# Graph attention on one core: the last batch's output summed on TensorE, and the last tile's masks placed in PSUM first

## The chip, the core and the metric

The kernel runs on one core of a Trainium2 chip. The metric is the device time of one execution in microseconds (us). Beside it stands a profile of one execution: the span from its first to its last instruction, and what each engine did in it. The engines are TensorE (PE; PEld is its weight load), VectorE (DVE), ScalarE (ACT), GpSimd (POOL) and SyncE (SP), which here only issues transfers. Each works through its own instructions in order and waits on semaphores for the others.

## The reference, cut to what matters

Sixteen batches (B), each with N = 512 nodes of F = 512 features, attend to their first 20 nodes, in two directions d, with 16 heads of 32 features. All inputs are float32.

```python
q_exp = jnp.where(row_zero[..., None], 0.0, q[:, None, :])
self_feat = jnp.concatenate([v, q_exp], -1) @ W_self.T + b_self
output = self_feat
for d in range(2):
    A = (adj_f if d == 0 else jnp.swapaxes(adj_f, 1, 2))[:, :, :20, :]
    cond = A.sum(-1)
    vb = A @ w_bias + b_bias
    kv = self_feat[:, :20]
    qh = (self_feat @ Wq[d].T + bq[d]).reshape(B, N, 16, 32)
    kh = (kv @ Wk[d].T + bk[d]).reshape(B, 20, 16, 32)
    aff = jnp.einsum('bnhd,bmhd->bnhm', qh, kh) / np.sqrt(32)
    aff = jnp.where(cond[:, :, None, :] > 0, aff, -9e15) + vb[:, :, None, :]
    w = softmax(aff, -1)
    out_t = jnp.einsum('bnhm,bmf->bnhf', w, kv)
    output += einsum('bnhf,hgf->bnhg', out_t, Wout[d]).reshape(B, N, 512) + bout[d]
return v + relu(output)
```

## The kernel before

**Setup.** Weights are folded: keys are brought into feature space (`g`), so that a score is one product of the self features with `g`; values (`vd`) already contain `Wout`. The biases `b_self` and `bout` are summed into `bo`, one number per output feature.

**Batches and tiles.** The main loop runs over batches `b` and over four tiles `nt` of 128 nodes. Everything is held with features on partitions: `xs[b]` and `sfs[b]` (self features without bias) are 128 partitions x 4 chunks x 512 nodes. A pass of the loop issues the products of the self features for later tiles (`self_feat`, L189), in pass 2 the attention of the batch before (`attend`, L314) and its output (`finish`, L327 and L333; `residual`, L336; `store`, L341), and then `scores` (L249) for this tile. There is no scheduler: the order in the source is the order on each engine, and the pools of tiles add waits.

**Scores and softmax.** A tile's scores fill two PSUM banks, one for each group `g` of 64 nodes; partitions are two halves of the heads times 64 nodes, and a bank's 320 columns are 8 heads x 40 neighbours (20 for each direction). One tile `ps_s` (pool `ps_s`, two buffers of two banks) holds both. `full` is the mask with the biases of that tile, made by POOL in `full_add` (L239) one pass ahead. `weigh` adds it to the scores in PSUM (L260), takes the maximum (L262) and subtracts it (L264); `expo` is the exponential on ScalarE (L269); in the next pass `normal` sums (L294), inverts (L295) and multiplies on POOL (L296), and `turn` (L303) transposes 32x32 blocks on VectorE into `wt`. For the last tile of the last batch, `weigh_half` and `turn_half` (L276 to L280, L285 to L288) do the same group by group and on VectorE.

**Attention.** `attend` multiplies `wt` with the values in 32x32 tiles of TensorE: 64 matmuls, which accumulate in pairs. Their results lie in four banks `q` (pool `ps_acc`, four buffers of one bank): `q // 2` gives the chunk pair, 0 and 1 or 2 and 3, and `q % 2` which 32 of every 64 nodes. Each bank is first written by a matmul with `start` set.

**The end.** The last batch has no successor, so its attention and output are written out after the loop, in two parts: tiles 0 to 2 (banks `most`), which wait for the transpose of tile 2, and tile 3 (banks `rest`), which waits for both halves of the last tile. VectorE adds the self features to the banks (L745), ScalarE adds `bo` and takes the ReLU (L749), POOL (L752) and VectorE (L755, L758) add `x`, and SP sends: three chunks of tiles 0 to 2 (L753), all chunks of tile 3 (L756), the fourth chunk (L759).

Of the kernel before, what the change touches and what calls it, by code (L numbers as in the profile page):

```python
# [13 lines left out]
P = 128  # L14
# [4 lines left out]
def gat_kernel(  # L19
# [224 lines left out]
    def scores(b, nt, g, ps):  # L244

        keys = gs[b].rearrange("p c (a w) -> p c a w", a=2)
        for k in range(C):
            for a in range(2):
                nc.tensor.matmul(  # L249
                    ps[bass.ts(a, R), g, : W // 2], sfs[b][:, k, bass.ds(nt * P + g * R, R)], keys[:, k, a],  # L250
                    start=(k == 0), stop=(k == C - 1),
                )
# [18 lines left out]
    def weigh_half(b, nt, ps, s, a):  # L271

        pw = ps[:, a, : W // 2]
        p3 = pw.rearrange("p (h m) -> p h m", m=NG)
        f = fulls[b, nt].rearrange("p g h m -> p g (h m)")[:, a]
        nc.vector.tensor_add(pw, pw, f)  # L276
# [28 lines left out]
    def attend(b, n, banks, tiles=slice(0, NT)):  # L305
# [3 lines left out]
        for i in range(2):  # L309
            for e in range(HL):  # L310
                j = n * HL * S // 32 + e * S // 32 + i
                for q in range(4):
# [4 lines left out]
                        start=(i == 0), stop=(i == 1),  # L317
# [314 lines left out]
    work = ctx.enter_context(tc.tile_pool(name="work", bufs=2))  # L632

    gs[0] = g0
    with tc.manual_schedule():
        load_keys(1)

# [3 lines left out]
        for b in range(B):  # L641
# [6 lines left out]

            for nt in range(NT):
# [21 lines left out]

                if prev is not None:
                    normal(*prev)
                ps = ps_s.tile([P, 2, 512], F32, tag="s", name=f"ps_s{b}_{nt}")
                for part in ahead(nt):
                    self_feat(*part)
                if nt == 2 and b > 0:
# [4 lines left out]
                    finish(b - 1, o, (0, 1), banks)  # L682
                for g in range(2):
                    scores(b, nt, g, ps)
# [11 lines left out]
                last = b == B - 1  # L696
                for part in ahead(nt):
                    self_copy(*part)
                if last and nt == NT - 1:
                    s = soft.tile(full, F32, tag="s", name=f"s{b}_{nt}", bufs=3)  # L700
                    weigh_half(b, nt, ps, s, 0)
                    turn(*prev)
                    weigh_half(b, nt, ps, s, 1)
                else:
                    s = weigh(b, nt, ps)
# [3 lines left out]
                if nt < NT - 1:  # L709
                    full_add(b, nt + 1)  # L710
# [16 lines left out]
        o = work.tile([P, C, N], F32, tag="o", name=f"o{b}")  # L727
        out_b = out[b].rearrange("(c p) n -> p c n", p=P)
        most = [ps_acc.tile([P, 512], F32, tag="acc", name=f"ps_o{b}_{q}") for q in range(4)]
        pairs = [ps_s.tile([P, 2, 512], F32, tag="s", name=f"ps_o{b}_{q}_2") for q in range(2)]  # L730
        rest = [pairs[q // 2][:, q % 2] for q in range(4)]
        parts = []
        for lo, hi, banks in ((0, NT - 1, most), (NT - 1, NT, rest)):
            width = (hi - lo) * R
            parts.append((slice(2 * lo, 2 * hi), slice(lo * P, hi * P), width, banks))
            for n in range(2):
                attend(b, n, [t[:, bass.ts(n, width)] for t in banks], slice(lo, hi))
        for ts, ns, width, banks in parts:
            for q in range(4):
                c = bass.ds(q // 2 * 2, 2)  # L740

                def of(t):
                    return t[:, c].rearrange("p c (t q n) -> p c t q n", q=2, n=32)[:, :, ts, q % 2]

                nc.vector.tensor_add(  # L745
                    of(o), banks[q][:, : 2 * width].rearrange("p (c t n) -> p c t n", c=2, n=32), of(sfs[b])
                )
            for c in range(C):
                nc.scalar.activation(o[:, c, ns], o[:, c, ns], AF.Relu, bias=bo[:, c : c + 1])  # L749
        ns = parts[0][1]  # L750
        for c in range(3):
            nc.gpsimd.tensor_add(o[:, c, ns], o[:, c, ns], xs[b][:, c, ns])  # L752
            nc.sync.dma_start(out_b[:, c, ns], o[:, c, ns])  # L753
        ns = parts[1][1]
        nc.vector.tensor_add(o[:, :, ns], o[:, :, ns], xs[b][:, :, ns])  # L755
# [50 lines left out]
```

## Time and profile before

| | |
|---|---|
| time, median of 3 runs (lowest to highest) | 634.22 us (633.94 to 636.79) |
| the profiled execution's own time | 634.41 us |
| its span | 632.6 us, mean granted TensorE clock 0.994 |
| busy, of the span | PE 98%, DVE 80%, POOL 53%, ACT 34% |
| chain that ended last | PE 85% (scores L249 43%, self features L189 33%, attention L314 6%) |
| the last batch's tile 2: scores on PE | start at 607.0 us |
| the last tile's second transpose on VectorE | 622.97 to 623.48 us |
| last send issued | 629.07 us |

"Busy" is the time in which an engine had an instruction of the program in work. The chain is followed back from the last instruction, at each step to what released it. A line of the timeline gives start, duration, engine, line of the kernel, operation, output and inputs, shape and count; in brackets how long the engine had idled and what ended that. The sum of an engine's durations can exceed its stretch a little, since instructions overlap at their ends. "Granted clock" is TensorE's clock as a share of full speed.

### The profile page before, as it was taken

How to read it: one execution, taken by the hardware profiler on the slowest of the kernel's cores; microseconds unless marked ns; L12 is line 12 of the kernel's file. 1: busy time of each engine (PE TensorE's matmuls, PEld its weight loads, DVE VectorE, ACT ScalarE, POOL GpSimd, SP SyncE). 2: the span in 40 equal slices, each digit the busy share in tenths (PEclk: the TensorE clock that was granted, in tenths of full speed). 3: DMA queues.
4: the chain of work that ended last, by engine and by line, in shares of the span. 5: the costliest groups of instructions: out<-in, count | busy, mean ns of one | idle time of the engine just before them, and what ended most of it. 6: DMA issues, size and time to landing. Idle time of an engine off the chain costs nothing.

```text
span 632.6 us, 16385 instructions
## 1 busy us (share of the span) xinstructions
PE 618.7 (98%) x6814; PEld 383.6 (61%) x6814; DVE 508.4 (80%) x815; ACT 218.1 (34%) x480; POOL 337.4 (53%) x258
## 2 busy tenths in 40 slices
PE   8999999999999999999999999999999999999993
PEld 6655459986565656565655656565656565656542
DVE  0566546879888888888888889797988888888886
ACT  1445321233342424242424233343334242424232
POOL 2405331446556464738392938474655646473853
PEclk9999999999999999999999999999999999999997
DMA  8999998628384565738392909292838465663322
GB/s 287 397 382 321 392 371 249 216 88 268 134 237 165 150 253 127 275 90 313 70 333 42 358 19 339 52 292 107 262 141 248 154 207 196 147 256 102 129 68 101
DMA packets 89569, 131.86 MB, mean 208 GB/s; under 512 B 8888, under 2 KB 59608, under 8 KB 87448
## 3 DMA queue, kind: packets, MB, share of 16 engines
q1 hardware_dynamic: 88824, 129.47, 61.7%
q0 software_dynamic: 672, 1.36, 0.8%
q8 instruction: 53, 0.87, 0.6%
q14 instruction: 20, 0.16, 0.1%
HBM read 90.89 MB, written 39.92 MB: 207 GB/s over the span
## 4 chain that ended last, share of the span: by engine, by line
PE 85%; DVE 2%; ACT 1%; issue 0%; DVEq 0%; ACTq 0%
PE ps_s L249 43%; PE ps_sf L189 33%; PE ps_o L314 6%; PE ps_v L523 1%; ACT o L749 0%; PE ps_nz L172 0%; DVE s L287 0%; DVE mx L278 0%; DVE o L745 0%; DVE s L279 0%; PE ps_g(3, 3, 0, 0, 2)0_778 L550 0%; PE ps_g(3, 2, 0, 1, 2)0_752 L550 0%; PE ps_g(3, 1, 1, 0, 2)0_724 L550 0%; PE ps_g(3, 0, 1, 1, 2)0_701 L550 0%; DVE ps_s L276 0%
## 5 line engine op out<-in xcount | busy, mean ns | idle before, releaser
L249 PE MATMUL ps_s<-g,sf 128*64 128x320 f32 x2048 | 287.6, 433 | 0.0
L249 PEld LDWEIGHTS ps_s<-g,sf 128*64 128x64 f32 x2048 | 155.4, 137 | 116.3 <-issue 6.2
L189 PE MATMUL ps_sf<-x,ws_v 128*64 128x256 f32 (+1 forms) x2048 | 222.0, 371 | 0.0
L189 PEld LDWEIGHTS ps_sf<-x,ws_v 128*64 128x64 f32 x2048 | 151.1, 137 | 67.5 <-issue 1.7
L296 POOL TENSOR_TENSOR s<-s,sm 128x640 f32<-128x640 f32 x63 | 80.1, 1271 | 145.5 <-DVE sm L295 134.8
L269 ACT ACTIVATE s<-s 128x640 f32<-128x640 f32 x63 | 46.5, 738 | 220.9 <-DVE s L264 220.9
L239 POOL TENSOR_TENSOR full<-cq,both 128x640 f32<-128x640 f32 x64 | 99.0, 1547 | 27.6 <-ACT both L230 23.5
L211 POOL TENSOR_TENSOR prod<-prod,wb_sb 128x880 f32<-128x880 f32 x32 | 61.3, 1915 | 56.5 <-ACT prod L210 56.5
L260 DVE TENSOR_TENSOR ps_s<-ps_s,full 128x640 f32<-128x640 f32 x63 | 52.3, 831 | 39.4 <-PE ps_s L249 39.4
L336 POOL TENSOR_TENSOR o<-o,x 128x512 f32<-128x512 f32 x60 | 75.5, 1281 | 0.0
L230 ACT COPY both<-add 64x80 f32<-64x80 f32 x128 | 32.8, 256 | 77.4 <-DVE add L225 76.3
L202 DVE SCALAR_TENSOR_TENSOR sf<-nz,qw,ps_sf 128x236 f32<-128x236 f32 (+1 forms) x128 | 52.6, 458 | 3.5 <-PE ps_sf L189 3.5
L333 ACT ACTIVATE o<-o,bo 128x512 f32<-128x512 f32 x60 | 40.0, 714 | 44.3 <-DVE o L327 44.3
L294 DVE TENSOR_REDUCE sm<-s 128x32 f32<-128x640 f32 x63 | 51.6, 818 | 4.4 <-ACT s L269 0.9
L262 DVE TENSOR_REDUCE mx<-ps_s 128x32 f32<-128x640 f32 x63 | 52.0, 825 | 2.2
L264 DVE TENSOR_TENSOR s<-ps_s,mx 128x640 f32<-128x640 f32 x63 | 51.9, 824 | 2.2
L303 DVE STREAM_TRANSPOSE wt<-s 128x640 f32<-128x640 f32 x63 | 52.5, 834 | 0.0
L314 PE MATMUL ps_o<-wt,vd 32*32 32x256 f32 (+2 forms) x2176 | 46.7, 381 | 4.2 <-issue 2.8
L314 PEld LDWEIGHTS ps_o<-wt,vd 32*32 32x32 f32 x2176 | 31.6, 104 | 19.8 <-issue 12.4
L327 DVE TENSOR_TENSOR o<-ps_o,sf 128x512 f32<-128x512 f32 x60 | 36.3, 668 | 0.0
L152 ACT ACTIVATE xn<-xn 128x512 f32<-128x512 f32 x56 | 34.3, 613 | 0.0
L216 DVE TENSOR_REDUCE cond<-adj 128x80 f32<-128x880 int32 x32 | 33.2, 1036 | 0.2 <-DMA adj<-in_adj 0.2
(205 smaller groups left out, 415.7 us busy)
## 6 DMA issues: line engine op xcount, KB each, us to landing
g<-g_d SPq DMA_DIRECT2D x15, 1280.0 KB, 9.0
g_d<-st SPq DMA_DIRECT2D x16, 1120.0 KB, 6.3
x<-in_xT SPq DMA_DIRECT2D x16, 1024.0 KB, 11.0
out_T<-o SPq DMA_DIRECT2D x61, 256.0 KB, 5.0
xn<-in_xn SPq DMA_DIRECT2D x28, 512.0 KB, 8.7
adj<-in_adj SPq DMA_DIRECT2D x32, 440.0 KB, 7.3
vd<-bd_d SPq DMA_DIRECT2D x64, 128.0 KB, 4.1
nz<-nz_d SPq DMA_DIRECT2D x14, 256.0 KB, 4.7
```

Of the source, the lines that this page charges most:

```text
L189: nc.tensor.matmul(held[0][bass.ts(a, R), i * N // 2 : i * N // 2 + hi - lo], ws_v[:, k, bass.ds((2 * f + i) * P + a * R, R)], xs[b][:, k, ...
L202: nc.vector.scalar_tensor_tensor(sfs[b][:, 2 * f + i, lo:hi], nzs[b][:, lo:hi], qw[:, 2 * f + i, b : b + 1], ps[:, i * N // 2 : i * N // 2 ...
L211: nc.gpsimd.tensor_mul(p, p, wb_sb.unsqueeze(1).to_broadcast([P, 2 * S, L]))
L239: nc.gpsimd.tensor_add(f, cqs[b].unsqueeze(1).to_broadcast(shape), adds[b, nt // 2][:, nt % 2].unsqueeze(2).to_broadcast(shape),)
L249: nc.tensor.matmul(ps[bass.ts(a, R), g, : W // 2], sfs[b][:, k, bass.ds(nt * P + g * R, R)], keys[:, k, a], start=(k == 0), stop=(k == C - 1),
L260: nc.vector.tensor_add(pw, pw, fulls.pop((b, nt)).rearrange("p g h m -> p g (h m)"))
L262: nc.vector.tensor_reduce(mx, p4, AX.X, ALU.max)
L264: nc.vector.tensor_sub(s, p4, mx.unsqueeze(3).to_broadcast(full))
L296: nc.gpsimd.tensor_mul(s, s, sm.unsqueeze(3).to_broadcast(full))
L303: nc.vector.transpose(wts[b][:, nt], s.rearrange("p a h m -> p (a h m)"))
L314: nc.tensor.matmul(banks[q][bass.ts(e, DH)].rearrange("p (t n) -> p t n", n=32), vds[b][r, e, i, q // 2 * 2 + n], wt[r, :, bass.ts(j, 32)] ...
L336: nc.gpsimd.tensor_add(o[:, c], o[:, c], xs[b][:, c])
```

## The change

- An identity matrix `ident` (128 x 128) is made on POOL in batch 1.
- In passes 0 and 1 of the last batch, ScalarE writes `biased` = self features + `bo`. POOL adds `x` to it: in chunks 0 and 1 for all nodes, in chunks 2 and 3 for the last tile's nodes only.
- For the last tile, each group of scores gets a bank of its own from `ps_acc`. `put_masks` writes the mask there by an identity matmul, and the scores accumulate on top; the mask add of `weigh_half` goes. The last mask sum is made on POOL one pass earlier, ahead of a `normal`.
- Each output bank of the last batch is started by `put_self`, an identity matmul of `biased`; `attend` accumulates on top (`start=False`). The one for bank 0 stands before the last tile's scores, the others behind them.
- Where the bank contains `x`, the output is the greater of bank and `x`, in one VectorE instruction: max(x + y, x) = x + relu(y). This holds for banks 0 and 1 of tiles 0 to 2 and all banks of tile 3. For banks 2 and 3 of tiles 0 to 2 ScalarE takes the ReLU from PSUM and POOL adds `x`.
- SP sends four pieces of two chunks each: tiles 0 to 2 (chunks 0 and 1, then 2 and 3), then tile 3 the same way. The output tile `o_last` takes a buffer of the keys, `biased` one of the outputs.

```diff
--- before.py
+++ after.py
@@ -241,14 +241,19 @@
             adds[b, nt // 2][:, nt % 2].unsqueeze(2).to_broadcast(shape),
         )
-    def scores(b, nt, g, ps):
+    def put_masks(b, nt, g, bank):
+        f = fulls[b, nt].rearrange("p g h m -> p g (h m)")
+        nc.tensor.matmul(bank[:, : W // 2], ident, f[:, g], start=True, stop=False)
+    def scores(b, nt, g, bank, start=True):
         keys = gs[b].rearrange("p c (a w) -> p c a w", a=2)
         for k in range(C):
             for a in range(2):
                 nc.tensor.matmul(
-                    ps[bass.ts(a, R), g, : W // 2], sfs[b][:, k, bass.ds(nt * P + g * R, R)], keys[:, k, a],
-                    start=(k == 0), stop=(k == C - 1),
+                    bank[bass.ts(a, R), : W // 2], sfs[b][:, k, bass.ds(nt * P + g * R, R)], keys[:, k, a],
+                    start=start and k == 0, stop=(k == C - 1),
                 )
     full = [P, 2, H, NG]
@@ -268,12 +273,9 @@
         sw = s.rearrange("p a h m -> p (a h m)")
         nc.scalar.activation(sw, sw, AF.Exp)
-    def weigh_half(b, nt, ps, s, a):
-        pw = ps[:, a, : W // 2]
-        p3 = pw.rearrange("p (h m) -> p h m", m=NG)
-        f = fulls[b, nt].rearrange("p g h m -> p g (h m)")[:, a]
-        nc.vector.tensor_add(pw, pw, f)
+    def weigh_half(b, nt, bank, s, a):
+        p3 = bank[:, : W // 2].rearrange("p (h m) -> p h m", m=NG)
         mx = soft.tile([P, H], F32, tag="mxh", name=f"mx{b}_{nt}{a}")
         nc.vector.tensor_reduce(mx, p3, AX.X, ALU.max)
         nc.vector.tensor_sub(s[:, a], p3, mx.unsqueeze(2).to_broadcast([P, H, NG]))
@@ -302,7 +304,7 @@
             wts[b] = work.tile([P, NT, W], F32, tag="wt", name=f"wt{b}")
         nc.vector.transpose(wts[b][:, nt], s.rearrange("p a h m -> p (a h m)"))
-    def attend(b, n, banks, tiles=slice(0, NT)):
+    def attend(b, n, banks, tiles=slice(0, NT), start=True, stop=True):
         wt = wts[b][:, tiles].rearrange("p t (g w) -> p (t g) w", g=2)
@@ -314,7 +316,7 @@
                     nc.tensor.matmul(
                         banks[q][bass.ts(e, DH)].rearrange("p (t n) -> p t n", n=32),
                         vds[b][r, e, i, q // 2 * 2 + n], wt[r, :, bass.ts(j, 32)],
-                        start=(i == 0), stop=(i == 1),
+                        start=start and i == 0, stop=stop and i == 1,
                     )
     def nodes(t, q):
@@ -630,10 +632,25 @@
     soft = ctx.enter_context(tc.tile_pool(name="soft", bufs=2))
     gp = ctx.enter_context(tc.tile_pool(name="gp", bufs=2))
     work = ctx.enter_context(tc.tile_pool(name="work", bufs=2))
+    ident = ctx.enter_context(tc.tile_pool(name="one", bufs=1)).tile([P, P], F32, name="ident")
     gs[0] = g0
     with tc.manual_schedule():
         load_keys(1)
+        def side(t, lo, hi, q):
+            v = t[:, bass.ds(q // 2 * 2, 2)].rearrange("p c (t q n) -> p c t q n", q=2, n=32)
+            return v[:, :, 2 * lo : 2 * hi, q % 2]
+        def of_bank(bank, lo, hi):
+            return bank[:, : 2 * (hi - lo) * R].rearrange("p (c t n) -> p c t n", c=2, n=32)
+        def put_self(banks, lo, hi, q):
+            nc.tensor.matmul(
+                of_bank(banks[q], lo, hi), ident, side(biased, lo, hi, q), start=True, stop=False
+            )
         prev = None
         o = None
@@ -646,6 +663,12 @@
                     return ((b, nt, 1),)
                 return ((b + 1, 0, 0), (b + 1, 1, 0)) if nt == 3 and b + 1 < B else ()
+            if b == 1:
+                nc.gpsimd.memset(ident, 0.0)
+                nc.gpsimd.affine_select(
+                    out=ident, in_=ident, pattern=[[-1, P]], compare_op=ALU.not_equal, fill=1.0,
+                    base=0, channel_multiplier=1,
+                )
             for nt in range(NT):
                 store()
                 if nt == 1:
@@ -669,9 +692,17 @@
                         load_xn(b + 2, 0)
                         load_xn(b + 2, 1)
+                if b == B - 1 and nt == 2:
+                    full_add(b, NT - 1)
                 if prev is not None:
                     normal(*prev)
-                ps = ps_s.tile([P, 2, 512], F32, tag="s", name=f"ps_s{b}_{nt}")
+                final = b == B - 1 and nt == NT - 1
+                if final:
+                    ps = [ps_acc.tile([P, 512], F32, tag="acc", name=f"ps_s{b}_{nt}{g}") for g in range(2)]
+                else:
+                    pair = ps_s.tile([P, 2, 512], F32, tag="s", name=f"ps_s{b}_{nt}")
+                    ps = [pair[:, g] for g in range(2)]
                 for part in ahead(nt):
                     self_feat(*part)
                 if nt == 2 and b > 0:
@@ -680,8 +711,17 @@
                         attend(b - 1, n, [t[:, bass.ts(n, N // 2)] for t in banks])
                     o = work.tile([P, C, N], F32, tag="o", name=f"o{b - 1}")
                     finish(b - 1, o, (0, 1), banks)
+                if final:
+                    o_last = gp.tile([P, C, W], F32, tag="g", name=f"o{b}")[:, :, :N]
+                    pair = ps_s.tile([P, 2, 512], F32, tag="s", name=f"ps_o{b}_0")
+                    most = [pair[:, q] for q in range(2)]
+                    most += [ps_acc.tile([P, 512], F32, tag="acc", name=f"ps_o{b}_{q}") for q in (2, 3)]
+                    put_self(most, 0, NT - 1, 0)
                 for g in range(2):
-                    scores(b, nt, g, ps)
+                    if final:
+                        put_masks(b, nt, g, ps[g])
+                    scores(b, nt, g, ps[g], not final)
                 if nt == 0 and b > 0:
                     mask_mul(b, 1)
@@ -693,21 +733,31 @@
                     mask_count(b + 1, 0)
                 if nt == 3 and b + 1 < B:
                     mask_add(b + 1, 0)
-                last = b == B - 1
                 for part in ahead(nt):
                     self_copy(*part)
-                if last and nt == NT - 1:
+                if b == B - 1 and nt < 2:
+                    if nt == 0:
+                        biased = work.tile([P, C, N], F32, tag="o", name="biased")
+                    for c in (2 * nt, 2 * nt + 1):
+                        nc.scalar.activation(biased[:, c], sfs[b][:, c], AF.Identity, bias=bo[:, c : c + 1])
+                if final:
                     s = soft.tile(full, F32, tag="s", name=f"s{b}_{nt}", bufs=3)
-                    weigh_half(b, nt, ps, s, 0)
+                    weigh_half(b, nt, ps[0], s, 0)
                     turn(*prev)
-                    weigh_half(b, nt, ps, s, 1)
+                    weigh_half(b, nt, ps[1], s, 1)
                 else:
-                    s = weigh(b, nt, ps)
+                    s = weigh(b, nt, pair)
                     expo(s)
                     if prev is not None:
                         turn(*prev)
                 if nt < NT - 1:
-                    full_add(b, nt + 1)
+                    if (b, nt + 1) not in fulls:
+                        full_add(b, nt + 1)
+                    if b == B - 1 and nt < 2:
+                        ns = slice(nt * (N - P), N)
+                        for c in (2 * nt, 2 * nt + 1):
+                            nc.gpsimd.tensor_add(biased[:, c, ns], biased[:, c, ns], xs[b][:, c, ns])
                 elif b + 1 < B:
                     full_add(b + 1, 0)
                 if nt >= 2 and b > 0:
@@ -724,39 +774,41 @@
         turn_half(*prev, 0)
         turn_half(*prev, 1)
-        o = work.tile([P, C, N], F32, tag="o", name=f"o{b}")
         out_b = out[b].rearrange("(c p) n -> p c n", p=P)
-        most = [ps_acc.tile([P, 512], F32, tag="acc", name=f"ps_o{b}_{q}") for q in range(4)]
-        pairs = [ps_s.tile([P, 2, 512], F32, tag="s", name=f"ps_o{b}_{q}_2") for q in range(2)]
-        rest = [pairs[q // 2][:, q % 2] for q in range(4)]
-        parts = []
-        for lo, hi, banks in ((0, NT - 1, most), (NT - 1, NT, rest)):
+        pair = ps_s.tile([P, 2, 512], F32, tag="s", name=f"ps_o{b}_0_2")
+        rest = [pair[:, q] for q in range(2)]
+        rest += [ps_acc.tile([P, 512], F32, tag="acc", name=f"ps_o{b}_{q}_2") for q in (2, 3)]
+        for lo, hi, banks, first in ((0, NT - 1, most, 1), (NT - 1, NT, rest, 0)):
+            for q in range(first, 4):
+                put_self(banks, lo, hi, q)
             width = (hi - lo) * R
-            parts.append((slice(2 * lo, 2 * hi), slice(lo * P, hi * P), width, banks))
             for n in range(2):
-                attend(b, n, [t[:, bass.ts(n, width)] for t in banks], slice(lo, hi))
-        for ts, ns, width, banks in parts:
-            for q in range(4):
-                c = bass.ds(q // 2 * 2, 2)
-                def of(t):
-                    return t[:, c].rearrange("p c (t q n) -> p c t q n", q=2, n=32)[:, :, ts, q % 2]
-                nc.vector.tensor_add(
-                    of(o), banks[q][:, : 2 * width].rearrange("p (c t n) -> p c t n", c=2, n=32), of(sfs[b])
-                )
-            for c in range(C):
-                nc.scalar.activation(o[:, c, ns], o[:, c, ns], AF.Relu, bias=bo[:, c : c + 1])
-        ns = parts[0][1]
-        for c in range(3):
-            nc.gpsimd.tensor_add(o[:, c, ns], o[:, c, ns], xs[b][:, c, ns])
-            nc.sync.dma_start(out_b[:, c, ns], o[:, c, ns])
-        ns = parts[1][1]
-        nc.vector.tensor_add(o[:, :, ns], o[:, :, ns], xs[b][:, :, ns])
-        nc.sync.dma_start(out_b[:, :, ns], o[:, :, ns])
-        ns = parts[0][1]
-        nc.vector.tensor_add(o[:, 3, ns], o[:, 3, ns], xs[b][:, 3, ns])
-        nc.sync.dma_start(out_b[:, 3, ns], o[:, 3, ns])
+                attend(b, n, [t[:, bass.ts(n, width)] for t in banks], slice(lo, hi), False, n == 1)
+        def end(lo, hi, banks, q):
+            nc.vector.tensor_max(side(o_last, lo, hi, q), of_bank(banks[q], lo, hi), side(xs[b], lo, hi, q))
+        def send(c, lo, hi):
+            nc.sync.dma_start(out_b[:, c : c + 2, lo * P : hi * P], o_last[:, c : c + 2, lo * P : hi * P])
+        for q in range(2):
+            end(0, NT - 1, most, q)
+        send(0, 0, NT - 1)
+        for q in (2, 3):
+            for n in range(2):
+                nc.scalar.activation(
+                    side(o_last, 0, NT - 1, q)[:, n], of_bank(most[q], 0, NT - 1)[:, n], AF.Relu
+                )
+        for n in (2, 3):
+            ns = slice(0, (NT - 1) * P)
+            nc.gpsimd.tensor_add(o_last[:, n, ns], o_last[:, n, ns], xs[b][:, n, ns])
+        send(2, 0, NT - 1)
+        for q in range(4):
+            end(NT - 1, NT, rest, q)
+            if q % 2:
+                send(q - 1, NT - 1, NT)
 def kernel(**inputs):
```

## The prediction

> **What bounds the kernel now.** I read the page first, for the balance of the engines and the chain that ended last, then the chain and the timeline of the last 30 us, then a table of windows over the same stretch for the granted clock.
>
> ```profile
> PE 618.7 (98%) x6814; PEld 383.6 (61%) x6814; DVE 508.4 (80%) x815; ACT 218.1 (34%) x480; POOL 337.4 (53%) x258
> ...
> PEclk9999999999999999999999999999999999999997
> ...
> PE 85%; DVE 2%; ACT 1%; issue 0%; DVEq 0%; ACTq 0%
> ```
>
> TensorE is busy 98% of the span and carries 85% of the chain, so for some 611 us the others wait for it. The change leaves its stream alone until then: the first PE instruction that differs comes after the scores of the last batch's tile 2. Only the last 21 us are in play, and there the timeline looks different (start, duration, engine, line):
>
> ```profile
> 616.18 0.47 DVE L276 TENSOR_TENSOR ps_s<-ps_s,full 128x320 f32<-128x320 f32 x1
> 616.41 1.27 POOL L296 TENSOR_TENSOR s<-s,sm 128x640 f32<-128x640 f32 x1 [1.89 <-DVE sm L295]
> ...
> 617.72 0.84 DVE L303 STREAM_TRANSPOSE wt<-s 128x640 f32<-128x640 f32 x1
> ...
> 618.66 3.64 PE L314 MATMUL ps_o<-wt,vd 32*32 32x192 f32 x128 [2.83 <-issue]
> ...
> 622.97 0.51 DVE L288 STREAM_TRANSPOSE wt<-s 128x320 f32<-128x320 f32 x1
> 623.41 2.82 DVE L745 TENSOR_TENSOR o<-ps_o,sf 128x384 f32<-128x384 f32 x8
> ...
> 623.63 1.66 PE L314 MATMUL ps_o<-wt,vd 32*32 32x64 f32 x128 [1.32 <-DVE wt L288]
> 624.42 3.30 ACT L749 ACTIVATE o<-o,bo 128x384 f32<-128x384 f32 x8 [3.92 <-DVE o L745]
> ...
> 629.07 0.53 SPq L759 DMA_DIRECT2D out_T<-o  x1
> ```
>
> PE has nothing to do for 2.8 us and again for 1.3 us; VectorE's softmax of the last tile runs without a gap from 616.18 to 623.48; then three passes over the output follow each other (VectorE add, ScalarE ReLU, an add of x on POOL or VectorE) until the last send at 629.07. It lands 2.2 us later, at 631.27; the span ends 1.33 us after that, at 632.6, and the execution took 634.41.
>
> ```profile
> core 0: us, PE busy (x) PEld busy (x) DVE busy (x) ACT busy (x) POOL busy (x), PEclk, DMA share, GB/s
> 615.80:618.00 2.20, 0.04 (x2) 0.00 (x0) 2.09 (x6) 0.20 (x1) 1.59 (x2) 1.00 0.13 50
> 618.00:618.50 0.50, 0.00 (x0) 0.00 (x0) 0.50 (x2) 0.27 (x1) 0.50 (x1) 0.58 0.00 0
> 618.50:621.40 2.90, 2.74 (x104) 2.59 (x105) 2.73 (x8) 0.47 (x1) 1.63 (x2) 0.50 0.37 145
> 621.50:622.30 0.80, 0.80 (x42) 0.43 (x24) 0.77 (x3) 0.00 (x0) 0.00 (x0) 1.00 0.20 72
> ```
>
> The idle 2.8 us cost PE its clock: 0.50 is granted from 618.5 to 621.4, most of the attention product over tiles 0 to 2.
>
> **The change, part by part.**
>
> *PE gets ten identity matmuls.* Four put the biased self features (384 columns) into banks before tiles 0 to 2 are attended, two put the masks (320) before the scores, four serve the last tile (128). Nearest rows, all with 128x128 weights; each matmul shows as two records:
>
> ```profile
> 3.78 1.06 PE L383 MATMUL ps_warm<-ones 128*128 128x128 f32 x4
> ...
> 14.81 0.96 PE L445 MATMUL ps_q<-sel,q 128*128 128x16 f32 x8
> ...
> 17.86 6.94 PE L472 MATMUL ps_k<-kvT,wk 128*128 128x320 f32 x24
> ```
>
> 320 columns: 6.94 / 12 = 0.58 us. 384 columns, scaled: 0.68 (below, 0.65 from the scores, whose pairs take 4.31 / 8 = 0.54 for 320; above, 1.29, two records of 644 ns of the 512-column L172). [...] Order on PE: self of bank 0, mask, scores of group 0, mask, scores of group 1, self of banks 1 to 3. From 611.50, where the last tile's scores started: 0.68 + 0.58 + 2.16 = 614.92 (group 0), + 0.58 + 2.16 = 617.66 (group 1), + 3 x 0.68 = 619.71. Before, scores ended at 615.84 and PE waited; now 2.8 us of it is filled, and tiles 0 to 2 start 1.05 us later than 618.66.
>
> *But they start at full clock.* Before, 3.64 us, of which about 2.83 at half clock: 3.64 - 1.42 = 2.22 warm. By widths, 256 columns took 2.76 and 64 took 1.66, so 192 would take 2.39. I take 2.3: end 622.01 against 622.30. [...] The row shows it halved after 2.2 us of idling (0.58 in 618.00 to 618.50). [...]
>
> Then four selfs of the last tile, 1.04: 623.05. What they wait for is long done: the banks of the scores are read by 619.5.
>
> *VectorE loses two mask adds (L276, 0.47 each, 0.50 with the gap).* The first buys nothing: the transpose at 617.72 needs POOL's product (L296, ends 617.68), so VectorE would only wait. The second counts: the last transpose ends at 622.98 instead of 623.48. Group 0 must be on hand at 616.18 (PE: 614.92) and group 1 at 618.5 (617.66): covers of 1.2 and 0.8 us; beyond them each us of PE delay is a us of VectorE delay.
>
> *Last tile's attention* starts at the later of 623.05 and 622.98 + 0.15 (the latency before), 623.13, and takes 1.66: 624.79 against 625.29.
>
> *Output.* Out go eight adds (L745), eight ReLUs (L749), the x adds. Banks 0 and 1 get one max each (0.50 a piece, as L745): 622.98 to 623.95, then a send, issued before the rest matters. Banks 2 and 3 of tiles 0 to 2 do not: they keep ReLU on ScalarE, four halves of 192 columns (between L749's rows of 606 and 388 ns: 0.44, pitch 0.36), from 622.10: third at 623.26, fourth at 623.62; then two POOL adds of 0.99 (pitch 0.96): 625.22. That is where the second send goes, at 625.25. The last tile's four maxes (284 ns, pitch 0.21) run from 624.9 to 625.8. SP is in order, so its two sends follow the POOL one, about 0.4 us apart (L756 to L759: 0.47): 625.65 and 626.05. Landing 2.2 us later: 628.25, against 631.27. Gain 3.02.
>
> *Costed at nothing.* Four ScalarE biasings (0.72 each, L333's row) stand ahead of the exponentials of tiles 0 and 1: done about 597.4 and 605.5, exponentials at 599.32 and 607.14; cover 1.7 us. POOL's x adds (two of 1.28, two of 128 columns, at most 0.99) end about 601.0 and 606.5. The last mask sum (L239, 1.55), moved ahead of a normalization, then ends near 608, before that normalization's sums are ready (609.12) and before PE wants it (612.2). Were POOL over 1 us late, that normalization, the transpose behind it and VectorE would shift. The identity (a memset and a select on POOL in batch 1; the 16-column select took 0.2, so 0.2 to 1.6) falls in the 4.9 us that POOL idles before 126.89. Its DMA waits are on setup stores issued by 93.75. The biased tile takes a slot of the output pair, so output 14 waits for output 13's stores: issued by 594.1 and needed at 609.04. SP sends four pieces for five.
>
> Sum: 634.41 - 3.02 = 631.4 for the profiled execution. That one lies 0.19 above the median of 634.22; against the median, 631.2. No change can be told apart from one within 0.5%, that is 631.05 to 637.39, so my sum lies almost on the edge.
>
> **The rivals.**
>
> *A smaller tail (631.2):* as worked out, own range 630.4 to 632.0.
>
> *B, PE is the bound:* the identity matmuls take the upper rows, or the half clock was not what made the 3.64. [...] For it: PE has only 0.08 us of room before the last tile. Against: the granted clock itself.
>
> *C, lighter sends:* the last two pieces are 128 KB, where before 256 and 192 KB shared the end. L753's pieces of 192 KB landed in 1.8, not 2.2; with SP issuing 0.35 apart that takes off 0.5: 630.7.
>
> *D, slower:* the self matmuls read runs of 32 elements with a stride. If PE streamed these at a quarter of the rate, the four of 384 columns cost 4 x 2.05 = 8.2 more and the four of 128 3.1 more: about 642. It turns the sign past +0.5% once the eight cost 6.2 us more than 3.8, that is beyond 2.6 times the contiguous price. Against: L314 also reads runs of 32, and 64 such matmuls of 256 columns took 2.76.
>
> That the change does not do what it says is half true and is in the sum: two of eight banks still go through ScalarE and POOL, and their POOL adds set the order of the sends.
>
> **How the numbers follow.** A 0.63, about half of it on each side of 631.05; C 0.17, all beyond; B 0.14, all within 0.5%; D 0.06. So faster 0.31 + 0.17 = 0.48, same 0.32 + 0.14 = 0.46, slower 0.06. The range runs from C's side, 630.1, to B's upper part, 633.2.
>
> **What would show it.** Right: PE without a gap from 611.5 to about 624.8, clock 1.00 throughout; tiles 0 to 2 attended in 2.2 to 2.4 us from about 619.7; the last L288 half a us earlier; POOL's last add near 625.2; last send near 626.1. Wrong: a half clock in that stretch, self matmuls over 0.8 us, a PE wait ahead of group 0's scores, VectorE waiting for either group, or any shift before 611 us.

## The result and the profile after

The changed kernel took 631.43 us (median of 10 runs, 630.05 to 634.12) beside 635.52 us (median of 10, 633.94 to 638.06) for the kernel before: a ratio of 0.9932, 95% interval 0.9916 to 0.9948. Measured once more beside other kernels it took 632.03 (11 runs, 630.17 to 637.36) against 634.55 (31 runs): 0.9960, interval 0.9936 to 0.9983. The profiled execution took 631.96, which is 2.45 below the one profiled before; its span is 630.0. Single executions of either kernel scatter by 4 to 7 us, and the one profiled before was a quick one. The predicted 631.2 is 0.2 from the first median, and both medians lie in its range of 630.1 to 633.2. As ratios, the first measurement lies beyond the half per cent on which the prediction put its border, the second within it; its nearly even chances are not decided by these two.

Part of that scatter sits in the body, where TensorE's work is the same in both kernels: VectorE's mask add of tile 2 (L260 before, L265 after) started at 611.65 before and at 611.95 after. From here on "tail" is the time from the start of that add to the end of the span. It is read within one execution, so the scatter of the body drops out of it; the two profiles of the changed kernel agree within 0.02:

| kernel | mask add of tile 2 | span | tail |
|---|---|---|---|
| before | 611.65 | 632.6 | 20.95 |
| after | 611.95 | 630.0 | 18.05 |
| after, second profile | 611.77 | 629.8 | 18.03 |

The tail lost 2.90; the prediction's sum was 3.02. The page after (balance of the engines, granted clock, chain that ended last):

```profile
PE 622.3 (99%) x6834; PEld 371.0 (59%) x6834; DVE 505.6 (80%) x809; ACT 218.2 (35%) x480; POOL 340.7 (54%) x263
...
PEclk9999999999999999999999999999999999999999
...
PE 87%; DVE 0%; issue 0%; DVEq 0%
```

VectorE's 2% and ScalarE's 1% of the chain are gone: TensorE now carries it almost to the end. The timeline of the tail after, for the stretch that was shown of before:

```profile
616.49 0.43 DVE L280 TENSOR_REDUCE mx<-ps_s 128x16 f32<-128x320 f32 x1
616.72 1.27 POOL L298 TENSOR_TENSOR s<-s,sm 128x640 f32<-128x640 f32 x1 [2.23 <-DVE sm L297]
...
618.02 0.84 DVE L305 STREAM_TRANSPOSE wt<-s 128x640 f32<-128x640 f32 x1 [0.58 <-POOL s L298]
...
618.49 2.20 PE L651 MATMUL ps_o<-biased,ident 128*128 128x384 f32 x6
...
620.62 2.33 PE L316 MATMUL ps_o<-wt,vd 32*32 32x192 f32 x128
...
622.74 0.51 DVE L290 STREAM_TRANSPOSE wt<-s 128x320 f32<-128x320 f32 x1
...
622.88 1.16 PE L651 MATMUL ps_o<-biased,ident 128*128 128x128 f32 x8
623.00 1.00 ACT L800 ACTIVATE o<-ps_o 128x192 f32<-128x192 f32 x4 [2.72 <-PE ps_o L316]
623.17 0.98 DVE L790 TENSOR_TENSOR o<-ps_o,x 128x384 f32<-128x384 f32 x2
623.85 1.95 POOL L805 TENSOR_TENSOR o<-o,x 128x384 f32<-128x384 f32 x2 [3.39 <-ACT o L800]
...
623.97 1.15 PE L316 MATMUL ps_o<-wt,vd 32*32 32x64 f32 x95
624.19 3.54 SPq L793 DMA_DIRECT2D out_T<-o  x4
...
625.74 0.48 PE L316 MATMUL ps_o<-wt,vd 32*32 32x64 f32 x33 [0.62 <-issue]
626.29 0.88 DVE L790 TENSOR_TENSOR o<-ps_o,x 128x128 f32<-128x128 f32 x4 [2.13 <-PE ps_o L316]
```

TensorE has no gap of 2.8 us and none of 1.3 us any more. The attention of tiles 0 to 2 takes 2.33 where it took 3.64, and where three passes over the output stood, six of the eight banks now take one and the other two take two. VectorE waits 0.58 for POOL's product ahead of L305, as the prediction had it for the first mask add. New is a gap of 0.62 us inside the last attention, released by nothing that the profile shows ("issue"); until TensorE is through, at 626.2, VectorE's last maxima cannot start. The granted clock, by the table of windows:

```profile
core 0: us, PE busy (x) PEld busy (x) DVE busy (x) ACT busy (x) POOL busy (x), PEclk, DMA share, GB/s
...
618.50:620.60 2.10, 2.10 (x8) 1.04 (x6) 2.00 (x6) 0.47 (x1) 1.96 (x2) 1.00 0.25 98
620.60:623.00 2.40, 2.40 (x130) 1.81 (x130) 2.26 (x6) 0.00 (x1) 0.00 (x0) 1.00 0.35 132
623.00:626.20 3.20, 2.58 (x136) 2.04 (x136) 1.16 (x3) 0.99 (x4) 1.95 (x2) 1.00 0.36 131
```

It is 1.00 throughout, also across the new gap. The same stretch as the chain of waits gives it, in order of time, is the list to hold against the prediction's steps (start, duration, what):

```profile
611.83 0.84 PE ps_o L651 x2
612.68 0.54 PE ps_s L247 x2
613.22 2.30 PE ps_s L254 x16
615.52 0.73 PE ps_s L247 x2
616.25 2.30 PE ps_s L254 x16
618.56 2.13 PE ps_o L651 x6
620.69 2.26 PE ps_o L316 x111
622.95 1.09 PE ps_o L651 x8
624.04 1.08 PE ps_o L316 x63
625.12 0.62 issue
625.74 0.57 PE ps_o L316 x25
```

### The profile page after: what moved, and what is told of

The parts are those of the page before. It is cut to its first block, busy times and chain, and to the rows that moved or that the text cites. A ratio compares the mean times of both kernels' runs of the same rounds, so it can differ in the third digit from the quotient of the medians.

```text
span 630.0 us, 16419 instructions
## 1 busy us (share of the span) xinstructions
PE 622.3 (99%) x6834; PEld 371.0 (59%) x6834; DVE 505.6 (80%) x809; ACT 218.2 (35%) x480; POOL 340.7 (54%) x263
## 4 chain that ended last, share of the span: by engine, by line
PE 87%; DVE 0%; issue 0%; DVEq 0%
PE ps_s L254 44%; PE ps_sf L189 33%; PE ps_o L316 7%; PE ps_v L525 1%; PE ps_o L651 1%; PE ps_s L247 0%; PE ps_nz L172 0%; PE ps_g(3, 1, 1, 0, 2)0_724 L552 0%; PE ps_g(3, 3, 0, 0, 2)0_778 L552 0%; PE ps_g(3, 2, 0, 1, 2)0_752 L552 0%; PE ps_g(3, 0, 1, 1, 2)0_701 L552 0%; PE ps_g(3, 0, 0, 0, 2)1_682 L552 0%; PE ps_g(3, 0, 0, 0, 2)0_681 L552 0%; DVE o L790 0%; PE ps_g(3, 3, 1, 1, 2)0_801 L552 0%
## 5 line engine op out<-in xcount | busy, mean ns | idle before, releaser
L254 PEld LDWEIGHTS ps_s<-g,sf 128*64 128x64 f32 x2048 | 145.6, 137 | 125.7 <-issue 7.1
L189 PEld LDWEIGHTS ps_sf<-x,ws_v 128*64 128x64 f32 x2048 | 146.6, 137 | 71.9 <-issue 1.7
L265 DVE TENSOR_TENSOR ps_s<-ps_s,full 128x640 f32<-128x640 f32 x63 | 52.3, 831 | 38.9 <-PE ps_s L254 37.4
L305 DVE STREAM_TRANSPOSE wt<-s 128x640 f32<-128x640 f32 x63 | 52.5, 834 | 0.6 <-POOL s L298 0.6
L316 PE MATMUL ps_o<-wt,vd 32*32 32x256 f32 (+2 forms) x2176 | 45.3, 372 | 0.6 <-issue 0.6
L316 PEld LDWEIGHTS ps_o<-wt,vd 32*32 32x32 f32 x2176 | 30.0, 103 | 16.1 <-issue 8.2
```

The source lines that it names most:

```text
L189: nc.tensor.matmul(held[0][bass.ts(a, R), i * N // 2 : i * N // 2 + hi - lo], ws_v[:, k, bass.ds((2 * f + i) * P + a * R, R)], xs[b][:, k, ...
L254: nc.tensor.matmul(bank[bass.ts(a, R), : W // 2], sfs[b][:, k, bass.ds(nt * P + g * R, R)], keys[:, k, a], start=start and k == 0, stop=(k ...
L265: nc.vector.tensor_add(pw, pw, fulls.pop((b, nt)).rearrange("p g h m -> p g (h m)"))
L305: nc.vector.transpose(wts[b][:, nt], s.rearrange("p a h m -> p (a h m)"))
L316: nc.tensor.matmul(banks[q][bass.ts(e, DH)].rearrange("p (t n) -> p t n", n=32), vds[b][r, e, i, q // 2 * 2 + n], wt[r, :, bass.ts(j, 32)] ...
```

## The experiments

Every ratio below is to the kernel before, timed on the same chip.

**1. Is the clock the reason for 2.3 in place of 3.64?** Kernel before, with five idle matmuls in TensorE's gap and nothing else:

```diff
+                if b == B - 1 and nt == NT - 1:
+                    fill = ps_acc.tile([P, 512], F32, tag="acc", name="ps_fill")
+                    for _ in range(5):
+                        nc.tensor.matmul(
+                            fill[:, : W // 2], sfs[b][:, 0, :P], gs[b][:, 0, : W // 2], start=True, stop=True
+                        )
```

> The kernel before with five matmuls of 320 columns, whose result nobody reads, in PE's idle time behind the last scores. Theory: PE does not idle for 2 us, the granted clock stays 1.00, tiles 0 to 2 are attended in 2.2 to 2.4 us in place of 3.64, and since VectorE's softmax (to 623.48) sets the output the span stays within 0.3 us of 632.6. Rival (such a gap costs no clock, and 3.64 us is the price of 192 columns): the attention keeps its 3.6 us.

Its timeline:

```profile
616.38 2.96 PE L688 MATMUL ps_fill<-g,sf 128*128 128x320 f32 x10
619.27 2.65 PE L314 MATMUL ps_o<-wt,vd 32*32 32x192 f32 x128
624.14 1.48 PE L314 MATMUL ps_o<-wt,vd 32*32 32x64 f32 x128 [2.23 <-DVE wt L288]
```

The granted clock of this stretch is 1.00 where 0.50 was granted before, and the same attention takes 2.65, which is 0.99 less. So the idling cost the clock, and the clock cost about 1 us. But 2.65 misses the expected 2.2 to 2.4: the clock is not the whole way from 3.64 to 2.33. The other 0.32 is gone in every kernel whose banks are started by the self matmuls (2.33 in "output only" too); what takes it off was not tried. The time did not change (635.4 us, 0.9998, interval 0.9984 to 1.0011; tail 21.04): in the kernel before, this us only lengthens TensorE's next wait, for VectorE's last transpose, from 1.3 to 2.2.

**2. The two parts alone.** "Output only": the change without its masks. Each score group starts its own bank, and VectorE adds the mask there.

```diff
-                    if final:
-                        put_masks(b, nt, g, ps[g])
-                    scores(b, nt, g, ps[g], not final)
+                    scores(b, nt, g, ps[g])
@@ weigh_half
+        f = fulls[b, nt].rearrange("p g h m -> p g (h m)")[:, a]
+        nc.vector.tensor_add(bank[:, : W // 2], bank[:, : W // 2], f)
```

> The change without its masks: the last tile's two mask adds are back on VectorE, the two mask matmuls are gone, the rest is as in the changed kernel. Theory (PE is the bound of the new tail): PE has 1.27 us less to do before the last tile's attention, VectorE 0.5 us more after the first add, which hides behind POOL's product; the last tile's attention starts 0.1 to 0.2 us earlier than in the changed kernel or at the same time, and the span is within 0.3 us of its 630.0. Rival (the masks carry part of the gain): VectorE is the bound, and the span is 0.5 to 1.0 us longer.

"Masks only": the kernel before, with `ident`, the earlier mask sum, the score groups in banks of their own and `put_masks`; its output stays as it was.

```diff
+                    if final:
+                        put_masks(b, nt, g, ps[g])
-                    scores(b, nt, g, ps)
+                    scores(b, nt, g, ps[g], not final)
@@ weigh_half
-        nc.vector.tensor_add(pw, pw, f)
```

> The kernel before with the masks alone: own banks and mask matmuls for the last tile, the output as before. Theory: the last L288 ends 0.5 us earlier (about 623.0), PE's scores end about 617.0, the output passes follow unchanged, so the span falls by 0.5 us at most, to about 632.1. Rival (the masks carry the gain): 1.5 us or more less than 632.6.

| kernel | us (runs) | ratio (interval) | tail | against 20.95 |
|---|---|---|---|---|
| output only | 633.44 (12) | 0.9979 (0.9960 to 0.9998) | 20.02 | -0.93 |
| masks only | 633.86 (12) | 0.9975 (0.9958 to 0.9992) | 20.45 | -0.50 |
| both (after) | 631.43 (10) | 0.9932 (0.9916 to 0.9948) | 18.05 | -2.90 |

The masks are worth the predicted 0.5. The output alone missed what was expected of it: its tail is 1.97 longer than the changed kernel's, where the theory left 0.3 and the rival 1.0. By the tails, from one profile of each part, the two add to 1.43, half of 2.90. The medians cannot tell: the parts take 0.21% and 0.25% off, the whole 0.68% or 0.40%. The lowest times side with the tails: the parts lie 1.2 and 0.5 us below the lowest of the kernel before, the whole 3.9 and 3.1. The timeline of "output only" shows one loss:

```profile
621.25 2.19 POOL L805 TENSOR_TENSOR o<-o,x 128x384 f32<-128x384 f32 x2 [1.97 <-ACT o L800]
621.29 0.25 DVE L290 RECIPROCAL sm<-sm 128x16 f32<-128x16 f32 x1
621.58 1.01 DVE L291 TENSOR_TENSOR s<-s,sm 128x320 f32<-128x320 f32 x1
```

VectorE's last softmax product, whose inputs both lie in SBUF, takes 1.01 us under POOL's adds; in every other place of these tails it takes 0.49. Without mask matmuls and scores waiting on them, the attention of tiles 0 to 2 ends earlier (9.57 us after tile 2's mask add, 11.00 in the changed kernel), so POOL's adds arrive while VectorE is still in the softmax: they start at 621.25, the last transpose at 622.62. In the changed kernel they start at 623.85, after that transpose (622.74 to 623.25). The other loss is among the sends: the first landed 4.1 us after its issue and the last 2.9 us (after: 2.5 and 1.9). Experiments 3 and 5 are about these two.

**3. The gap of 0.62 us.** Counting TensorE's recorded entries (weight loads, matmuls, semaphores), the gap stands in front of number 13762 in the changed kernel and in "masks only", although the last attention begins elsewhere in the two. That speaks for the stream of instructions. By the page's queue "q8 instruction: 53, 0.87" MB a packet has 16 KB (0.87 MB / 53), and 13831 entries over 53 packets are 261 each. The 256 entries with which the expectations below reckon are not shown by that mean; the run with 50 idle matmuls tests them. A gap that comes from the fetch of such a packet is called a fetch stop from here on. To move the border, idle matmuls go into the set-up, 42 or 50 of them, four entries each:

```diff
+            for i in range(42):
+                r = bass.ts(i % 4, 32)
+                nc.tensor.matmul(warm[r, :32], ones[r, :32], ones[r, :32], start=True, stop=True)
```

> The changed kernel with 42 idle 32x32 matmuls more in the set-up of TensorE (168 more entries in its instruction stream, nothing else). Theory (instruction fetch): the 0.62 us stall of the last attention stands in front of TensorE's recorded entry 13762 in three kernels whose attention has another number of matmuls ahead of it, and the entry 256 earlier had run only 3.1 to 3.7 us before; so it is the wait for the next 256 instructions. 168 entries more put this border near the 20th entry of the last attention and the one before it near the 40th entry of tiles 0 to 2's, some 3.3 us earlier: stall 0 to 0.2 us, the last attention ends 0.4 to 0.6 earlier, and from VectorE's mask add of tile 2 to the end of the span 17.4 to 17.7 instead of 18.05. Rival (a wait of the product itself: a bank, a row group, the clock): the gap of 0.62 stays after the 95th record, 18.05. The set-up may take up to 1 us more, so the whole time says less than the tail.

> The changed kernel with 50 idle matmuls in TensorE's set-up instead of 42 (32 entries more than the last kernel). Theory (instruction fetch): the border now falls some 12 entries ahead of the end of the last attention, and the border before it into the self matmuls at about 623.3; with 3.1 to 3.7 us from one to the other at least, the last few matmuls wait 1.0 to 1.5 us, and the attention ends 0.3 to 0.6 later than in the changed kernel: 18.4 to 18.7 from the mask add of tile 2 to the end, about 1.0 more than with 42. Rival (a wait of the product itself): no difference between 42, 50 and the changed kernel beyond 0.1, the gap after the 95th record.

> The changed kernel once more, beside the three others on the same chip: 631.4 within 0.5 if the first measurement holds, and again a stall of 0.5 to 0.7 us in front of the same entry of TensorE's stream if it belongs to the instruction stream; a stall that comes and goes from one execution to another would speak for the rival.

With 42 the last attention runs through (timeline):

```profile
624.93 1.48 PE L316 MATMUL ps_o<-wt,vd 32*32 32x64 f32 x128
```

With 50 it stops, and in another place:

```profile
623.37 1.43 PE L316 MATMUL ps_o<-wt,vd 32*32 32x64 f32 x123
625.43 0.30 PE L316 MATMUL ps_o<-wt,vd 32*32 32x64 f32 x5 [0.63 <-issue]
```

This stop stands ahead of entry 14018 = 13762 + 256, near the end as expected: the two stops are 256 entries apart. The second profile of the changed kernel stops for 0.55 ahead of 13762 again. The gap belongs to the instruction stream, then, and the rival is out. The entry behind a stop ran 2.2 to 2.9 us after the start of its packet in all eight profiles with a stop over 0.1 (2.34 in the changed kernel: packet 623.40, entry 625.74), and 1.2 to 1.5 after its end. The 1.0 to 1.5 us expected with 50 were too many: 0.63.

The tails missed what was expected of them (17.4 to 17.7 with 42, 18.4 to 18.7 with 50): they are 18.28 and 18.15, no better than 18.05 (632.52 us in 11 runs, 0.9959, interval 0.9944 to 0.9974, and 632.61 in 10, 0.9959, 0.9943 to 0.9976). With 42 the third send goes out 0.45 us earlier against tile 2's mask add (14.41 for 14.86), and this is lost behind it. The DMA view of the last us with 42 (queues, then KB each and median us to landing):

```profile
q1 hardware_dynamic: 1090, 1.05, 37.8%
q8 instruction: 1, 0.02, 1.1%
...
out_T<-o SPq DMA_DIRECT2D x2, 384.0 KB, 3.5
out_T<-o SPq DMA_DIRECT2D x2, 128.0 KB, 2.4
```

and with 50, from the first send on:

```profile
q1 hardware_dynamic: 1088, 1.05, 39.6%
issues: line engine op xcount, KB each, median us to landing
out_T<-o SPq DMA_DIRECT2D x2, 384.0 KB, 2.5
out_T<-o SPq DMA_DIRECT2D x2, 128.0 KB, 1.9
```

With 42 the next packet of instructions falls among the sends (625.39, the sends at 625.15 to 627.84), with 50 none does, and the landings differ by 1.0 and 0.5 us. The split is the same in all kernels with four sends: a packet among them in "output only", in this one and in two below, first pieces landing after 3.5 to 4.1 us; none in the six other profiles, 2.5 us. The last two kernels of experiment 6, which differ in the padding alone, fall on the two sides. Where a packet was among the sends of "output only", the rate at the end of the DMA view is some 20 GB/s for over a us, while 350 to 400 flowed before:

```profile
GB/s 0 0 0 0 0 9 413 359 350 369 369 397 350 359 406 369 388 406 152 19 110 334 328 107 296 356 161 19 28 19 22 19 22 19 0 0 0 0 0 0
```

By an estimate from this row, that is about one of the 16 DMA engines still working (a sixteenth of 350 to 400 is 22 to 25). Whether it is the one that also carried the instructions, no run shows.

**4. Does POOL's add set the order of the sends?** The prediction said so. Here VectorE finishes all four banks of tiles 0 to 2:

```diff
-                        ns = slice(nt * (N - P), N)
+                        ns = slice(0, N)
@@ the end
-        for q in range(2):
+        for q in range(4):
             end(0, NT - 1, most, q)
-        send(0, 0, NT - 1)
-        ... four halves on ScalarE, two adds on POOL
-        send(2, 0, NT - 1)
+            if q % 2:
+                send(q - 1, 0, NT - 1)
```

> The changed kernel with all four banks of tiles 0 to 2 finished by one maximum each on VectorE; ScalarE's halves and POOL's adds at the end are gone (the x is put into the self term for all columns, off the path). Theory (TensorE's last product sets the last sends): the second send goes out up to 0.7 earlier (625.1 for 625.8), the third and fourth do not move, and the time from tile 2's mask add to the end stays at 18.05 within 0.2. Rival (the prediction's step that POOL's add sets the order of the sends): the last two sends and the end come 0.4 to 0.7 earlier.

Measured: 631.7 us (12 runs, 0.9950, interval 0.9934 to 0.9966), tail 17.73. Against tile 2's mask add the second send goes out 0.72 earlier (13.16 for 13.88), the third and fourth 0.39 earlier (14.47 for 14.86), more than the 0.2 that TensorE's theory left. The chain says why:

```profile
624.16 1.08 PE ps_o L316 x63
625.24 0.24 issue
625.47 0.57 PE ps_o L316 x25
626.04 0.27 DVE o L790
```

The fetch stop is 0.24 here, not 0.62. The third send follows the end of TensorE's last matmul by 0.6 us in both kernels (625.92 and 626.54; 626.21 and 626.81). TensorE sets the last sends, and the 0.39 is the shorter stop. Its packet was through 12.10 us after tile 2's mask add, for 12.43 in the changed kernel, though by the timeline the attention of tiles 0 to 2 starts 8.67 after it in both. Why the packet came earlier was not tried; it may be scatter, since the second profile of the changed kernel has it at 12.26 and a stop of 0.55. POOL's add takes over only where TensorE is done early: with the 42 idle matmuls TensorE ended at 626.41, POOL at 626.76, and the third send, queued behind POOL's, went out at 627.33, 0.9 after TensorE.

**5. Is it POOL that stretches the product?** "Output only" with the edit of experiment 4:

> The kernel with the change to the output alone (masks still added on VectorE, before the softmax), and all four banks of tiles 0 to 2 finished by VectorE's maximum: ScalarE's halves and POOL's adds at the end are gone. [...]

The product takes 0.49 again where it took 1.01 under POOL's adds, so they cost it 0.52 us; by what means, no run shows. The tail falls from 20.02 to 19.29: the author expected 19.1 to 19.6 if POOL's adds were the cause, 19.9 to 20.1 if not (634.67 us in 12 runs, 0.9985, interval 0.9966 to 1.0004, so the timed runs show no gain over "output only"). A packet of instructions lies among the sends of this kernel too (first landing after 3.95 us), so most of its distance to 18.05 is left.

**6. Toward a better version.** Group 0's mask back on VectorE, where it only fills the wait for POOL; then with experiment 4; then with the 42 idle matmuls as well.

```diff
@@ weigh_half
+        if a == 0:
+            f = fulls[b, nt].rearrange("p g h m -> p g (h m)")[:, a]
+            nc.vector.tensor_add(bank[:, : W // 2], bank[:, : W // 2], f)
@@ scores of the last tile
-                    if final:
+                    if final and g == 1:
                         put_masks(b, nt, g, ps[g])
-                    scores(b, nt, g, ps[g], not final)
+                    scores(b, nt, g, ps[g], not (final and g == 1))
```

> The changed kernel with group 0's mask added by VectorE again, and only group 1's put there by a matmul. Theory: the add takes 0.5 us of the time in which VectorE waits for POOL's product anyway (0.58 us), PE has 0.65 us less, so the last tile's attention starts about 0.6 us earlier and the span falls to about 629.4. Rival (VectorE is the bound): no gain, or 0.5 us longer.

> The changed kernel with group 0's mask added on VectorE and all four banks of tiles 0 to 2 finished there too. TensorE theory: the single edits brought 0.6 and 0.4 off the tail, of which 0.3 to 0.4 is each time the shorter fetch stall (0.28 and 0.24 for 0.62); together the tail is 17.2 to 17.5 (from 18.05), the span about 629.3, if the stall is 0.2 to 0.3 again. Rival (POOL's add orders the sends): the two gains add to 1.0, tail 17.0.

> The last kernel with the 42 idle matmuls in TensorE's set-up. Fetch theory: no stall in the last attention (128 records in 1.48 us), its end 0.2 to 0.3 earlier against tile 2's mask add than without the 42. With the POOL adds gone nothing else orders the last sends, so they go out 0.2 to 0.3 earlier too; but the next fetch of instructions falls among the sends (as it did with the 42 in the changed kernel, where the last landing took 2.4 us instead of 1.9), so the tail is 17.0 to 17.4. Rival (with the 42, the sends were held by POOL's add alone, and the fetch beside them costs nothing): 16.8 to 17.0.

| kernel | us (runs) | ratio (interval) | tail | fetch stop |
|---|---|---|---|---|
| mask of group 0 on VectorE | 631.69 (6) | 0.9938 (0.9918 to 0.9957) | 17.43 | 0.28 |
| and all maxima on VectorE | 631.22 (12) | 0.9952 (0.9935 to 0.9969) | 17.23 | 0.11 |
| and 42 idle matmuls | 633.44 (12) | 0.9970 (0.9953 to 0.9987) | 18.44 | 0.13 |

The first two came out as expected. In the second the last transpose still ends 11.29 us after tile 2's mask add, as it does after the change (11.30): VectorE lost nothing. It has the shortest span of all, 628.8, and a tail 0.8 below that of the changed kernel, 0.5 of it the shorter stop, for which experiment 4's caution holds; the timed runs cannot tell the two apart. The third missed its 17.0 to 17.4. A stop of 0.13 remained, and a packet at 626.20 fell among the sends: first landing after 3.7 us, last after 2.9 (2.5 and 2.1 without). That costs more than the stop of 0.11 that the 42 were to remove.

## Why the prediction was right, step by step

Times from the start of tile 2's mask add, predicted (from 611.65) and measured (from 611.95):

| step | predicted | measured |
|---|---|---|
| group 0's scores done | 3.27 | 3.57 |
| group 1's scores done | 6.01 | 6.61 |
| attention of tiles 0 to 2 starts | 8.06 | 8.74 |
| and takes | 2.30 | 2.26 |
| last transpose ends | 11.33 | 11.30 |
| last attention starts | 11.48 | 12.09 |
| last attention ends | 13.14 | 14.36 |
| POOL's adds end | 13.57 | 13.85 |
| last send issued | 14.40 | 15.32 |
| last piece landed | 16.60 | 17.18 |
| end of the span | 17.93 | 18.05 |

- *Full clock for tiles 0 to 2*: right, 2.26 for 2.3 at a granted clock of 1.00. 3.64 at full clock did not occur in any run: at 1.00 the same attention took 2.26 after the change and 2.65 in experiment 1. The working was right in part only. It took 1.42 off for the clock, and experiment 1 shows 0.99; that the length still came out is luck, owed to the other 0.32, whose cause stays open.
- *Two mask adds*: right to 0.03, the first worth nothing, the second 0.5.
- *Costed at nothing* (biasing, x adds, the mask sum moved ahead): nothing of it showed; TensorE's tail begins 0.12 before the mask add, as against 0.15.
- *TensorE's identity matmuls*: mis-sized. The self of bank 0 took 0.84 for 0.68, over the 0.8 that the prediction named as a sign of being wrong; the two masks 0.54 and 0.73 for 0.58 each, the scores behind them 2.30 for 2.16, three selfs 2.13 for 2.04, the last four 1.09 for 1.04. With the 0.04 won in the attention and 0.03 at the start that makes 0.68, and the room of 0.08 was used up at once: the "tie" between TensorE and VectorE was won by TensorE by 0.6. Rival B's price for this (selfs of 1.29) did not occur, but its claim that TensorE becomes the bound did. No run shows the extra time behind B's upper part and the range's upper end of 633.2, nor the 0.26 a piece behind the predicted 1.04: the last four selfs took 0.27 each (1.09 / 4), and the attention of tiles 0 to 2 took 2.26.
- *Last attention, 1.66*: this is the term that was mis-sized most. The product takes 1.48 where no fetch stops it (experiments 1 and 3); it took 2.27 here, from 624.04 to 626.31: 0.79 more, of which the stop shows 0.62. TensorE without a gap, a sign the prediction named of being right, did not come. In the kernel before the same packet of instructions came at 622.48, while TensorE idled 1.3 us, and only a pause of 0.19 was left of the stop, at the same place of the stream (624.76 to 624.95); the 1.66 held it unseen. Taking the idle stretch away took away what hid the fetch.
- *POOL's add sets the order of the sends*: wrong. TensorE's end does: the third send follows it by 0.6 us with POOL's adds and without them (experiment 4).
- *Landing of 2.2 us, and 1.33 behind it*: both too long, by 0.34 and 0.42. The last piece of 128 KB landed in 1.86, which is rival C's thought. After the landing SP works off the program's closing waits, 0.06 us each; in the kernel before, seven of them stood behind the one for the landing (631.33 to 631.78), after the change it was the last of them (629.15), so the end followed 0.9 us later.
- *Rival D* (strided reads at a quarter of the rate): out. A self matmul of 384 columns takes 0.71 (2.13 / 3).

So the tail's sum was right within 0.12 because two misses met, which is luck: the last send came 0.92 late, and 0.8 less stood behind it. The 0.2 between 631.43 and the predicted 631.2 is luck as well. The prediction took 3.02 off a median of three runs, 634.22, while ten gave 635.52; as a gain, 3.02 stands beside 4.09 in the first measurement and 2.52 in the second.

What made 2.90 of parts worth 0.93 and 0.50? In "output only", the product under POOL (0.52) and a last landing of 2.95 for 1.86 (1.09) lose 1.6 that the masks, by moving POOL's adds and the fetch out of the way, gave back; experiments 3 and 5 show each by itself, and their sum is about the 1.47 missing. No run took both out of "output only", so that they make up the whole of it is arithmetic, not shown.

## What to carry to other kernels

When work is moved into an engine's idle stretch, ask what that stretch was hiding: here it hid an instruction fetch of 2.2 to 2.9 us, which the last attention's 1.5 us of short matmuls could not cover. Judge a tail of a few us from a fixed point in the trace of the same execution, beside the medians, and from more than one profile where a fetch falls into it. Test the parts of a change both alone and together: by their tails, the parts here were worth half of the whole. A padding that shifts the fetch can cost more at its new place than it saves at the old one (here a tail of 18.44 for 17.23), so look where the next packet falls.

## What the runs showed of the hardware

- TensorE stopped 0.11 to 0.63 us at a fixed place of its instruction stream (ahead of entry 13762; with 200 entries more in the set-up, ahead of 14018, 256 later), in 32x32 matmuls that use up 256 entries in 1.5 us. Its packets of instructions were of 16 KB, 261 entries each in the mean (13831 / 53).
- With a packet of instructions among the four output sends, the first landed after 3.5 to 4.1 us (2.5 without) and the last after 2.4 to 2.9 (1.8 to 2.1 without).
- VectorE's product of two SBUF inputs (128x320, float32) took 1.01 us while POOL added beside it, and 0.49 without (experiments 2 and 5).
- SP's closing waits cost 0.06 us each behind the landing that comes last: 0.42 us in the kernel before.
